# Four short runs of quarter-width products per pair of batches gathered into two

## The chip, the cores and the metric

The kernel runs on one core of one Trainium2 chip. The metric is the device time of one execution, in microseconds (us). TensorE multiplies, VectorE and ScalarE work on what it leaves in PSUM and prepare weights, GpSimd sets a few constants at the start, and SyncE's queue (SP) issues nearly all transfers.

## The reference, cut to what matters

Eight batches of 256 tokens with 1024 features go through four layers, each added to the residual stream:

```python
x = x + (x @ W0.T + 2 * lora(x, gates(x @ Wr.T)))       # 8 experts of rank 16, top 2 of 8 logits
x = x + (x @ W1.T + b1 + coeff[b] * (x @ (2 * mask[b] - 1)))
x = x + x @ W2[ids[b]].T                                # a weight per adapter
x = x + (x @ B3[ids[b]].T) @ A3[ids[b]].T               # adapter of rank 16
```

The router's logits `x @ Wr.T` (8 columns) decide which two experts of layer 0 a token uses. The projections `x @ B3[id].T` (16 columns) are the first half of layer 3. These two small products, both in float32, are what the change moves.

## The kernel before, in words

The residual stream is kept transposed, features on partitions, in K = 8 blocks of 128 features by T = 256 tokens. float32 operands of the large products are split into a high and a low float32r part, and a product is taken as high x high + high x low + low x high. `three` (lines 408 to 423) does so for the two batches of a pair at once, 512 tokens wide: 16 products with the weight's high part (L412, L413), then 8 with its low part (L420). `two` (425 to 439) does it for one batch: 8 products of the high part with both parts of x (L428), then 8 of 256 tokens with the low part (L436). Each takes callbacks: `early`, `mid` (between the high and the low part) and `late` (behind the low part) put other products of TensorE at these places.

The batches are taken in four pairs, q = 0 to 3. A pair is a stream of units, one weight block of 128 x 1024 each: one unit A (all experts' first factors, 128 rows), 8 units L0 (output block m), 16 units L1 and 16 units L2 (block m, batch j of the pair). Units are numbered through: with pair 0, A is 0, L0 is 1 to 8, L1 is 9 to 24, L2 is 25 to 40, so that unit (m, j) = (4, 1) of layer 2 is 34, (6, 0) is 37, and pair 1's A is 41. `slot(i)` issues a unit's work in a fixed order: the load of unit i + 9, the evacuation of the last unit's products, the high and low parts (L184 on ScalarE, L191 on VectorE) of units about four ahead, the addition of the identity to later blocks (`fold`, L159 on VectorE, five and six units ahead), other side work, and then `main(i)`, the unit's products. The order on each engine is the order in which the program is written; nothing is planned at run time. Loads of weights, masks, and inputs share ten buffers of the pool "raw"; a load waits on SP's queue until its buffer is let go by its last reader.

Logits and projections have few output columns. They are padded to 32, a quarter of the array: `logits(b, h)` takes half of batch b's eight feature blocks, four products that go to the four quarters of the array (L259), from the raw input; two halves finish a batch. `proj(b, h)` does the same for the adapter's projections from the finished x of layer 2 (L467). The four quarters' results are four partial sums, on 32 partitions each. The logits' are copied (L265), transposed (L270), and summed by `router` on VectorE. The projections' are split (`proj_sum`, L90 on ScalarE and L91 on VectorE) and summed by a product with a constant (`sums`, L369 and L370), which `rank` puts into the middle of the next pair's first L0 unit. Products with float32 operands stand in the trace as two records each.

For a pair that has a next one, with n = 2q + 2 the next pair's first batch, `main` puts them as follows: in the middle of unit (4, 1) of layer 2 the first halves of both batches' projections and all logits of batch n; in the middle of (6, 0) the logits of n + 1; in the middle of the next A the second half of the first batch's projections; behind that A the second half of the other's. The results lie in buffers of the PSUM pool "aux", four of 512 floats by 128 partitions. At the start the first pair's logits come as the input comes, and the last pair has places of its own.

Of the kernel before, what the change touches and what calls it, by code (L numbers as in the profile page):

```python
# [8 lines left out]
F32 = mybir.dt.float32  # L9
# [6 lines left out]
P = 128  # L16
NB = 8          # batches
T = 256         # tokens of a batch
K = 8           # blocks of 128 features
E = 8           # experts / adapters  # L20
R = 16          # rank
LOAD_AHEAD = 9  # weight blocks loaded, and prepared, ahead of their products
PREP_AHEAD = 4
MERGE_AHEAD = (6, 7)    # layer 1's blocks merged before the layer: the first pair's, the others'
W1_BUFS = 3
RAW_BUFS = 10
WARM = 9        # products that raise the tensor engine's clock
# prepared later, so that the vector engine is free where layer 2 waits for layer 1's results
# [4 lines left out]
def kernel(ctx: ExitStack, tc: tile.TileContext, x, lang, coeff, ids,  # L33
                           mask, w0, wr, la, lb, w1, b1, w2, a3, b3, out):
    """The residual stream is kept transposed (features on partitions), so that each
    layer's output is the next one's moving operand. float32 operands are split
    exactly into two float32r parts (hi: 12 bits, lo: the rest)."""
    nc = tc.nc
# [11 lines left out]
    aux = ctx.enter_context(tc.tile_pool(name="aux", bufs=4, space=PS))  # L50
# [4 lines left out]
    # ---- small constants  # L55
    xraw = {}

    def load_x(b, h, parts=1):
        """Half of batch b's input."""
        t = rawp.tile([P, K // 2, T], F32, tag="raw", name=f"x{b}_{h}")  # L60
        n = K // 2 // parts
        for i in range(parts):
            c = slice(i * n, (i + 1) * n)
            nc.sync.dma_start(t[:, c, :], x[b, :, h * K // 2 + i * n:h * K // 2 + (i + 1) * n, :])
        xraw[b, h] = t

    # the router's weights: 8 columns and 24 of zeros, a quarter of the array's
# [8 lines left out]
    # the sum over the array's quarters, of R rows each, as three copies  # L76
# [11 lines left out]
    # ---- splits  # L88
# [19 lines left out]
    # ---- the stream of weight blocks, in the order of use  # L108
    units = []
    for q in range(NB // 2):  # L110
        units.append(("A", q, 0, 0))
        units += [("L0", q, m, 0) for m in range(K)]
        units += [("L1", q, m, j) for m in range(K) for j in range(2)]
        order = [(m, j) for m in range(K) for j in range(2)]
        if q == NB // 2 - 1:        # the last pair's first batch ends sooner
            order[-6:] = [(m, j) for j in range(2) for m in range(K - 3, K)]
        units += [("L2", q, m, j) for m, j in order]
    raws, ws, w1raw = {}, {}, {}

    def parts(i):  # L120
        # the first blocks come in two parts
        n = 2 if i < 2 else 1
        return [slice(j * K // n, (j + 1) * K // n) for j in range(n)]
# [26 lines left out]
    # a block's preparation in four steps, on two engines in turns  # L150
# [6 lines left out]
    def add_identity(w, m):  # L157
        """The residual, in the block where inputs and outputs are the same."""
        nc.vector.tensor_tensor(w[:, m, :], w[:, m, :], ident, ALU.add)  # L159
# [43 lines left out]
    # first blocks, ahead of the other constants  # L203
# [26 lines left out]
    def constants():  # L230
        # 5 where the expert is the batch's language; ids below 0 match none
        lang_f = cst.tile([P, NB], F32, name="lang_f")
        nc.vector.tensor_scalar(lang_f, lang_i, -1.0, float(E), ALU.mult, ALU.add)
        nc.vector.tensor_tensor(bias, rev.to_broadcast([P, NB, E]),
                                lang_f.rearrange("p (b o) -> p b o", o=1)
                                      .to_broadcast([P, NB, E]), ALU.is_equal)
        nc.vector.tensor_scalar(bias, bias, 5.0, None, ALU.mult)
        nc.vector.tensor_scalar(c2, c_sb, 2.0, None, ALU.mult)
        nc.vector.tensor_scalar(negc, c_sb, -1.0, None, ALU.mult)
        # adapters as an index: from the end below 0, then held in range  # L240
        neg = cst.tile([1, NB], F32, name="neg")
        idf = cst.tile([1, NB], F32, name="idf")
        nc.vector.tensor_scalar(neg, ids_raw, 0.0, float(E), ALU.is_lt, ALU.mult)
        nc.vector.tensor_tensor(idf, ids_raw, neg, ALU.add)
        nc.vector.tensor_scalar(ids_sb, idf, 0.0, float(E - 1), ALU.max, ALU.min)

    # ---- layer 0's router, from logits [16 = hi|lo, 512 tokens]
# [4 lines left out]
    def logits(b, h):  # L252
        """Half of batch b's logits in float32, four blocks of features at a time in the
        quarters of the array."""
        q, j = divmod(b, 2)
        if (j, h) == (0, 0):
            pls[q] = aux.tile([P, 512], F32, tag="aux", name=f"pl{q}")
        for g in range(4):
            nc.tensor.matmul(pls[q][32 * g:32 * g + 32, j * T:(j + 1) * T],  # L259
                             wrs[:, 4 * h + g, :], xraw[b, h][:, g, :],  # L260
                             start=(h == 0), stop=(h == 1))
# [11 lines left out]
    def router(q, pt):  # L273
# [31 lines left out]
        # 2 (the scaling) over 1 + e, and e times that  # L305
# [28 lines left out]
    # ---- layer 3, per batch  # L334
# [20 lines left out]
    def proj_sum(b, pb):  # L355
        """The sum over the quarters, three times."""
        pr = aux.tile([P, 512], F32, tag="aux", name=f"pr{b}")
        if b == NB - 1:
            # in one step, as nothing else is left to do meanwhile
            raw = gp.tile([P, T], F32, tag="pbraw", name="pbraw")  # L360
            nc.scalar.copy(raw, pb[:, :T])
            return pr, lambda: nc.tensor.matmul(pr[:96, :T], sel3_raw, raw, start=True,
                                                stop=True)
# [9 lines left out]
    def third(b, pb):  # L373
        """The projections' rows as hi, lo and hi again."""
        rt = l3p.tile([96, T], FR, tag="rt", name=f"rt{b}")
        nc.scalar.copy(rt, pb[:96, :T])
        nc.vector.tensor_tensor(rt[32:64, :], pb[32:64, :T], f32(rt[32:64, :]), ALU.subtract)
        return rt
# [17 lines left out]
    # ---- products  # L396
# [11 lines left out]
    def three(po, hi, lo, xhi, xlo, last=True, early=(), mid=(), late=()):  # L408
        """po = (hi + lo)^T (xhi + xlo), over the K blocks of 128; early, mid, late:
        other work in between."""  # L410
# [14 lines left out]
    def two(po, hi, lo, xhl, early=(), mid=(), late=()):  # L425
        """As three(), for one batch: hi with x's both parts at once, into po's halves."""
# [21 lines left out]
    summed = []     # units whose two halves' sum is under way  # L448
    done = []       # what is left of the units that have gone through the tensor engine
# [11 lines left out]
    def proj(b, h):  # L461
        """Half of batch b's projections onto its adapter's rank, in float32 and the
        quarters of the array."""
# [14 lines left out]
    def first_products():  # L478
        """The first two units' products and the first logits, as the input comes in."""
# [20 lines left out]
        for j in range(2):  # L500
# [15 lines left out]
            # both halves stay open, for the experts' part, in one group that batch 0 starts  # L516
# [11 lines left out]
    def main(i):  # L528
        """Unit i on the tensor engine."""
# [6 lines left out]
        if kind == "A":  # L536
            xhi, xlo = x0[q]
            ph = aux.tile([P, 512], F32, tag="aux", name="ph")
            three(ph, hi, lo, xhi, xlo, mid=[lambda: proj(b - 2, 1)],
                  late=[lambda: proj(b - 1, 1)])  # L540
            phs[q] = ph
        elif kind == "L0":
# [12 lines left out]
            if m == 1:  # L555
                def gate_now():
                    gates[q] = gate(gxs.pop(q), phs.pop(q))
                # the first gates come later than the others
# [15 lines left out]
        else:  # L574
            xh = hls[2, b]
            po = ps.tile([P, 512], F32, tag="mm", name=f"po2_{b}_{m}")
            if (m, j) == (4, 1):
                mid = [lambda: proj(b - 1, 0), lambda: proj(b, 0)]
            if q < NB // 2 - 1:
                n = 2 * q + 2  # L580
                if (m, j) == (4, 1):
                    mid += [lambda: logits(n, 0), lambda: logits(n, 1)]
                if (m, j) == (6, 0):
                    mid = [lambda: logits(n + 1, 0), lambda: logits(n + 1, 1)]
# [4 lines left out]
            else:  # L589
                if (m, j) == (K - 3, 1):  # L590
                    mid = [lambda: proj(b - 1, 1)]
# [4 lines left out]
            if i == len(units) - 1:  # L596
                # its sum is waited for at once
# [10 lines left out]
    nxt = []        # work for the vector engine once the scalar engine's is done  # L608

    def side(i):  # L610
        """Other loads and preparations beside unit i's products."""
# [19 lines left out]
    # the tensor engine's clock rises while the first blocks come in  # L631
# [8 lines left out]
    # the slots in which layer 1's weights are merged: the more in layer 0's, which leave the  # L640
    # vector engine time
# [8 lines left out]
    def slot(i):  # L650
        """Unit i's products, beside the evacuation of those before it and the
        preparation of those after it."""
# [14 lines left out]
        # the next products wait for the last ones' results: nothing between  # L667
# [28 lines left out]
    def evacuate(between=None):  # L696
        """Products (and bias) split into the next ones' operand."""
        items = done[:]
        done.clear()
        # those summed beside the last unit, then those complete on PSUM  # L700
# [27 lines left out]
    # the last batch's end: half of the residual joins on the tensor engine, so that two  # L728
    # engines can take the sums
# [81 lines left out]
```

## Time and profile before

| | us |
|---|---|
| Median of 3 runs | 628.63 (628.33 to 628.91) |
| Span of the profiled execution | 627.1 |
| Median less that span | 1.5 |
| TensorE busy, of the span | 618.9 (99%) |
| TensorE loading weights | 521.9 (83%) |
| VectorE busy | 460.6 (73%) |
| ScalarE busy | 362.9 (58%) |
| L467, 128 records of 32 x 256 | 9.9 |
| L259, 128 records of 32 x 256 | 9.5 |
| Clock granted to TensorE, mean | 0.997 of full speed |

The span goes from the first to the last instruction of one profiled execution on the core; the runs' time holds what lies around it as well. PE is TensorE's products and PEld its weight loads, which lie beside products. DVE is VectorE and ACT ScalarE; SPq is the queue of SyncE. A product's modelled end lies after the next one's start, so the sum of busy times counts some time twice; the distance from start to start is what a product costs. In a row of the timeline, "x8" is the number of records merged into it. "128*32" is the weight's shape, "128x256 f32" that of the moving operand. What stands in brackets behind a row is the engine's idle time before it, and who ended that.

### The profile page before, as it was taken

To read this page: it belongs to the slowest core of one execution; us is meant where nothing else is said; L and a number is where in the kernel's file an instruction comes from. 1 tells how busy PE (TensorE), PEld (TensorE's weight loads), DVE (VectorE), ACT (ScalarE), POOL (GpSimd) and SP (SyncE) were. 2 spreads that over 40 slices of the span, in tenths; PEclk is the share of its full clock that TensorE was granted. 3 is DMA by queue.
4 is the path that set the end of the run, shared out by engine and by line. 5 is a ranking of instruction groups with operands and counts; after the bars stand their busy time and mean duration, and the time that the engine had idled before them with its cause. 6 is when DMAs were issued, how large, how long until landed. Compare 5 with 4: busy or idle time off the path is not lost.

```text
span 627.1 us, 9247 instructions
## 1 busy us (share of the span) xinstructions
PE 618.9 (99%) x3458; PEld 521.9 (83%) x3458; DVE 460.6 (73%) x800; ACT 362.9 (58%) x552; POOL 1.0 (0%) x14
## 2 busy tenths in 40 slices
PE   8999999999999999999999999999999999999996
PEld 6888888888788888888878888888787888888885
DVE  6685898766657799777666689967775678987642
ACT  5375797565354498655435558865534446975521
POOL 0000000000000000000000000000000000000000
PEclk9999999999999999999999999999999999999998
DMA  8974575668725776476842778647774358765104
GB/s 272 397 229 153 201 269 174 208 203 270 250 72 168 234 268 199 138 247 220 310 136 74 203 240 276 186 138 247 240 272 134 121 182 259 247 199 164 39 0 135
DMA packets 38815, 125.01 MB, mean 199 GB/s; under 512 B 4722, under 2 KB 5874, under 8 KB 38770
## 3 DMA queue, kind: packets, MB, share of 16 engines
q1 hardware_dynamic: 38626, 124.15, 60.4%
q8 instruction: 27, 0.44, 0.3%
q10 hardware_dynamic: 144, 0.26, 0.1%
q14 instruction: 18, 0.15, 0.1%
HBM read 116.01 MB, written 8.39 MB: 198 GB/s over the span
## 4 chain that ended last, share of the span: by engine, by line
PE 98%; DMA 1%; SPq 0%; DVE 0%; ACT 0%; DVEq 0%; issue 0%
PE po L428 37%; PE po L436 20%; PE po L412 9%; PE po L420 9%; PE po L413 9%; PE pb L467 1%; PE po L454 1%; PE po L455 1%; PE po L456 1%; PE pl L259 1%; PE po L388 1%; PE ph L420 1%; PE ph L413 1%; PE ph L412 1%; DMA raw<-in_la 1%; PE ph L489 0%
## 5 line engine op out<-in xcount | busy, mean ns | idle before, releaser
L428 PE MATMUL po<-hl,whi 128*128 128x512 f32 x1016 | 254.5, 392 | 0.0
L428 PEld LDWEIGHTS po<-hl,whi 128*128 128x128 f32 x1016 | 182.9, 189 | 32.9
L191 DVE TENSOR_TENSOR wlo<-raw,whi 128x1024 fp32r<-128x1024 f32 (+1 forms) x166 | 199.0, 1205 | 1.8 <-ACT whi L184 1.8
L184 ACT CAST whi<-raw 128x1024 fp32r<-128x1024 f32 (+1 forms) x166 | 172.4, 1039 | 10.5 <-DVE raw L159 8.1
L436 PEld LDWEIGHTS po<-hl,wlo 128*128 128x128 f32 x1016 | 137.7, 190 | 12.2 <-issue 3.3
L436 PE MATMUL po<-hl,wlo 128*128 128x256 f32 x1016 | 142.7, 283 | 0.0
L412 PE MATMUL po<-x0hi,whi 128*128 128x512 f32 x248 | 97.1, 392 | 0.0
L413 PE MATMUL po<-x0lo,whi 128*128 128x512 f32 x248 | 96.7, 390 | 0.0
L174 DVE TENSOR_TENSOR raw<-raw,w 128x1024 f32<-128x1024 f32 x64 | 78.1, 1221 | 3.6 <-ACT raw L154 2.6
L154 ACT ACTIVATE raw<-raw,negc,c 128x1024 f32<-128x1024 int32 x64 | 79.7, 1245 | 0.0
L711 ACT COPY xt<-po 128x256 f32<-128x256 f32 x63 | 23.4, 372 | 87.2 <-PE po L436 87.2
L720 DVE TENSOR_TENSOR xt<-po,xt 128x256 f32<-128x256 f32 x63 | 26.7, 423 | 50.6 <-ACT xt L711 50.3
L420 PE MATMUL po<-x0hi,wlo 128*128 128x512 f32 x248 | 62.3, 393 | 0.0
L704 ACT CAST hl<-po 128x256 fp32r<-128x256 f32 x64 | 20.5, 376 | 71.6 <-PE po L456 71.5
L718 DVE TENSOR_TENSOR hl<-po,hl 128x256 fp32r<-128x256 f32 x64 | 23.8, 420 | 46.1 <-ACT hl L704 40.7
L412 PEld LDWEIGHTS po<-x0hi,whi 128*128 128x128 f32 x248 | 46.6, 188 | 11.1 <-issue 1.2
L413 PEld LDWEIGHTS po<-x0lo,whi 128*128 128x128 f32 x248 | 46.6, 188 | 9.8
L420 PEld LDWEIGHTS po<-x0hi,wlo 128*128 128x128 f32 x248 | 45.4, 188 | 8.8
L714 ACT ACTIVATE sum<-po,b_sb 128x256 f32<-128x256 f32 x64 | 30.4, 475 | 23.4 <-PE po L436 23.1
L720 DVE TENSOR_TENSOR sum<-po,sum 128x256 f32<-128x256 f32 x64 | 26.8, 419 | 12.7 <-ACT sum L714 12.6
L718 DVE TENSOR_TENSOR hl<-sum,hl 128x256 fp32r<-128x256 f32 x64 | 26.8, 419 | 4.6 <-ACT hl L704 4.6
L704 ACT CAST hl<-sum 128x256 fp32r<-128x256 f32 x64 | 25.6, 400 | 7.6 <-DVE sum L720 7.6
(116 smaller groups left out, 379.9 us busy)
## 6 DMA issues: line engine op xcount, KB each, us to landing
raw<-in_w SPq DMA_DIRECT2D x95, 512.0 KB, 4.3
raw<-in_mask SPq DMA_DIRECT2D x64, 512.0 KB, 5.4
w<-in_w SPq DMA_DIRECT2D x32, 512.0 KB, 4.6
out<-xt SPq DMA_DIRECT2D x31, 256.0 KB, 3.1
x<-in_x SPq DMA_DIRECT2D x12, 512.0 KB, 4.4
a3raw<-in_a SPq DMA_DIRECT2D x8, 384.0 KB, 3.6
x<-in_x SPq DMA_DIRECT2D x8, 256.0 KB, 5.8
raw<-in_la SPq DMA_DIRECT2D x3, 512.0 KB, 3.6
```

The costliest lines, as they stand in the source:

```text
L154: nc.scalar.activation(f32(raws[i]), raws[i], AF.Identity, bias=negc[:, b:b + 1], scale=c2[:, b:b + 1])
L174: nc.vector.tensor_tensor(s, s, w1raw[q, m], ALU.add)
L184: nc.scalar.copy(hi[:, c], source(i)[:, c])
L191: nc.vector.tensor_tensor(lo[:, c], source(i)[:, c], f32(ws[i])[:, c], ALU.subtract)
L412: nc.tensor.matmul(po, hi[:, k, :], xhi[:, k, :], start=(k == 0), stop=False)
L413: nc.tensor.matmul(po, hi[:, k, :], xlo[:, k, :], start=False, stop=False)
L420: nc.tensor.matmul(po, lo[:, k, :], xhi[:, k, :], start=False, stop=(last and k == K - 1))
L428: nc.tensor.matmul(po, hi[:, k, :], xhl[:, k].rearrange("p h t -> p (h t)"), start=(k == 0), stop=False)
L436: nc.tensor.matmul(po[:, :T], lo[:, k, :], xhl[:, k, 0, :], start=False, stop=(k == K - 1))
L704: nc.scalar.copy(hi, p)
L718: nc.vector.tensor_tensor(lo, p, f32(hi), ALU.subtract)
L720: nc.vector.tensor_tensor(xs, p[:, :T], xs, ALU.add)
```

## The change

For the first three pairs all logits of the next pair, of both batches, go into the middle of unit (6, 0), and nothing into (4, 1). All projections of both batches go behind the next unit A, nothing into its middle: `proj(b, None)` takes all eight blocks of a batch in one go, and ends with `proj_sum` as the second half did. The start, and the last pair with its places (4, 1), (5, 1) and the end, stay. The rest of the diff takes out comments and blank text.

```diff
     def proj(b, h):
+        if h is None:
+            pbs[b] = aux.tile([P, 512], F32, tag="aux", name=f"pb{b}")
+            for k in range(K):
+                g = k % 4
+                nc.tensor.matmul(pbs[b][32 * g:32 * g + 32, :T], l3[b][1][:, k, :],
+                                 xts[b][:, k, :], start=(k < 4), stop=(k >= 4))
+            prs[b], sums[b] = proj_sum(b, pbs.pop(b))
+            return
         if h == 0:
             pbs[b] = aux.tile([P, 512], F32, tag="aux", name=f"pb{b}")
...
         if kind == "A":
             xhi, xlo = x0[q]
             ph = aux.tile([P, 512], F32, tag="aux", name="ph")
-            three(ph, hi, lo, xhi, xlo, mid=[lambda: proj(b - 2, 1)],
-                  late=[lambda: proj(b - 1, 1)])
+            three(ph, hi, lo, xhi, xlo, late=[lambda: proj(b - 2, None), lambda: proj(b - 1, None)])
             phs[q] = ph
...
             po = ps.tile([P, 512], F32, tag="mm", name=f"po2_{b}_{m}")
-            if (m, j) == (4, 1):
-                mid = [lambda: proj(b - 1, 0), lambda: proj(b, 0)]
             if q < NB // 2 - 1:
                 n = 2 * q + 2
-                if (m, j) == (4, 1):
-                    mid += [lambda: logits(n, 0), lambda: logits(n, 1)]
                 if (m, j) == (6, 0):
-                    mid = [lambda: logits(n + 1, 0), lambda: logits(n + 1, 1)]
+                    mid = [lambda: [logits(bb, h) for bb in (n, n + 1) for h in range(2)]]
                 if (m, j) == (6, 1):
                     l2s[q + 1] = logits_by_token(q + 1)
                 if (m, j) == (7, 0):
                     mid = [l2s[q + 1][1]]
             else:
+                if (m, j) == (4, 1):
+                    mid = [lambda: proj(b - 1, 0), lambda: proj(b, 0)]
                 if (m, j) == (K - 3, 1):
                     mid = [lambda: proj(b - 1, 1)]
```

The buffers follow from the new order: a batch's projection buffer in "aux" is now taken behind A, where it was held from (4, 1) on, and the raw buffers of batch n's input are held up to (6, 0).

## The prediction

> **What bounds the kernel now.** I read the page's busy row first, then the chain that ended last.
>
> ```profile
> PE 618.9 (99%) x3458; PEld 521.9 (83%) x3458; DVE 460.6 (73%) x800; ACT 362.9 (58%) x552; POOL 1.0 (0%) x14
> PE 98%; DMA 1%; SPq 0%; DVE 0%; ACT 0%; DVEq 0%; issue 0%
> ```
>
> TensorE is busy for 99% of the span and makes up 98% of the chain. So a change counts here only by what it does to the distance between one product's start and the next on TensorE. Busy time can't show that distance, since a product's modelled end overlaps its successor; start times can. The timeline of TensorE around the first pair's layer 2 has these rows (start, length, engine, line, tiles, form, records):
>
> ```profile
> 136.52 2.00 PE L428 MATMUL po<-hl,whi 128*128 128x512 f32 x8
> 138.46 1.07 PE L467 MATMUL pb<-xt,b 128*32 128x256 f32 x16
> 139.34 1.05 PE L259 MATMUL pl<-x,wrs 128*32 128x256 f32 x16
> ...
> 141.37 2.00 PE L428 MATMUL po<-hl,whi 128*128 128x512 f32 x8
> ...
> 144.16 2.00 PE L428 MATMUL po<-hl,whi 128*128 128x512 f32 x8
> ...
> 146.96 2.00 PE L428 MATMUL po<-hl,whi 128*128 128x512 f32 x8
> 148.89 1.07 PE L259 MATMUL pl<-x,wrs 128*32 128x256 f32 x16
> ...
> 150.95 2.00 PE L428 MATMUL po<-hl,whi 128*128 128x512 f32 x8
> ```
>
> A unit of layer 2 without anything in it lasts from 144.16 to 146.96, 2.80 us. The unit that holds eight projection and eight logits products (each stands in the trace as two records, so 16 + 16) lasts from 136.52 to 141.37, 4.85 us: 2.05 more. The unit with eight logits products (16 records) lasts from 146.96 to 150.95, 3.99 us: 1.19 more. Sixteen further records thus cost 0.86, or 0.054 us each, and the run itself costs 1.19 - 16 x 0.054 = 0.33 us, however long it is. I call a stretch of quarter-width products (the form 128*32) between full-width ones a run, and the 0.33 its fixed price.
>
> The two short runs, of four projection products each, check this. They stand in the next unit, A:
>
> ```profile
> 159.76 0.40 PE L412 MATMUL ph<-x0hi,whi 128*128 128x512 f32 x1
> ...
> 163.19 0.39 PE L413 MATMUL ph<-x0lo,whi 128*128 128x512 f32 x1
> 163.51 0.64 PE L467 MATMUL pb<-xt,b 128*32 128x256 f32 x8
> 164.08 2.11 PE L420 MATMUL ph<-x0hi,wlo 128*128 128x512 f32 x8
> 166.12 0.64 PE L467 MATMUL pb<-xt,b 128*32 128x256 f32 x8
> 166.69 0.50 PE L412 MATMUL po<-x0hi,whi 128*128 128x512 f32 x1
> 167.03 0.39 PE L413 MATMUL po<-x0lo,whi 128*128 128x512 f32 x1
> ```
>
> From 159.76 to 163.19 are 15 starts, 0.229 apart. Unit A's 24 products would take 24 x 0.229 = 5.49 us; it lasts until 166.69, 6.93 us. The first product behind the second run is followed after 0.34 (167.03) and not 0.23, another 0.11. So the two runs cost 1.55, 0.77 each; the rule above gives 0.33 + 8 x 0.054 = 0.76. The fixed price shows at the edges: 0.32 us from the last full-width start to the run's first (163.19 to 163.51) and not 0.23, and 0.34 behind the run's first successor; the rest is between the run's last records and that successor.
>
> **The change, part by part.**
>
> *Runs on TensorE.* Per pair that has a next one (three of the four) the runs are now 32, 16, 8 and 8 records. After the change they are 32 (all logits, in unit (6,0) of layer 2) and 32 (all projections, behind A's products). No product goes or comes: 64 records on both sides. Before: 2.05 + 1.19 + 1.55 = 4.79 us. After: 2 x 2.05 = 4.10 us. The difference, 0.69, is two fixed prices (2 x 0.33 = 0.67). I take 0.67 per pair; the other two pairs show the same row lengths (1.07, 1.05, 1.07, 0.64, 0.64), so 3 x 0.67 = 2.0 us. The start-up and the last pair keep their runs.
>
> A rule speaks against this. The Trainium skill's "TensorE: Matmul & The Clock Gate", section "Measured speedup vs the span model", prices a pack of products in different parts of the array at one product's duration plus about 4 ns for each further one. With the trace's 0.379 us for L467's records that is 0.39 per pack of four. If packs simply stood one behind another, the 16 packs of a pair would cost 16 x 0.39 = 6.3 us in two runs as in four, and the saving would be 0. The rows say otherwise: 16 records, four packs, take 139.34 - 138.46 = 0.88 us, 0.22 each. Packs of one run overlap; it is the edges that are paid in full. So 2.0 by the rows, 0 by the rule; I take the rows.
>
> *A semaphore wait within a run.* In the changed kernel's order of instructions, batch b - 1's first projection waits for its adapter's load and for its PSUM buffer, and one of these waits became an instruction of its own on TensorE's queue, amid the run. Both are long fulfilled: the load by a whole layer, the buffer (the logits' before) by the scalar engine's copy of them, three units earlier. Such instructions exist already:
>
> ```profile
> L412 PEldq EVENT_SEMAPHORE  x4: 51/51/51, 38.3 to 56.5; - x4
> ```
>
> The first, at 38.3, lies between products that start at 37.96, 38.18, 38.41 and 38.64: no gap, as the queue runs ahead. None in the trace lies within a quarter-width run. From both sides: nothing, or, if the run falls into two, one more fixed price, 0.33 per pair and 1.0 in all. I take 0, by the row, and keep 1.0 for the range.
>
> *Later projections, and who waits.* The first projections move from mid A to its end, so their splits move too. Now:
>
> ```profile
> 164.27 0.37 ACT L90 CAST pbhi<-pb 128x256 fp32r<-128x256 f32 x1 [0.44 <-PE pb L467]
> 166.85 0.37 ACT L90 CAST pbhi<-pb 128x256 fp32r<-128x256 f32 x1 [2.21 <-PE pb L467]
> 167.26 0.42 DVE L91 TENSOR_TENSOR pblo<-pb,pbhi 128x256 fp32r<-128x256 f32 x1 [1.11 <-ACT pbhi L90]
> ```
>
> The scalar engine waits for the second projections anyway; nothing stands between its two splits. On the new clock, A's end comes at 166.12 - 2.05 + 0.86 - 0.77 = 164.16 (logits gone from (4,1), more of them in (6,0), no run in mid A). The run's halves finish at about 165.4 and 166.3 (start, 0.88 per half, some 0.4 for a product to end). Then the splits: ScalarE to 166.7, VectorE to about 167.1, which is 0.5 sooner than now (167.68). What stands behind them, the high and low parts of later weights, moves up with them. The sums (L369, L370) come 16 products after the run, at 164.16 + 1.85 + 16 x 0.229 = 169.7: 2.6 us of cover. Without it each microsecond would be paid on TensorE, three times. The batch's last block of layer 2, which the last projection reads, is done at 164.48 - 1.2 = 163.3, and is read at 165.5.
>
> *One batch's logits three units later.* No DMA instruction moves, but two of the four "raw" buffers (of ten) that hold the next inputs are let go later, and the weights behind them on SP's queue change buffers. Now:
>
> ```profile
> SPq L144 <- PE pl L259: 11.3, 7, 2.8
> DMA to landing us min/median/max: 3.3/4.7/6.9
> ```
>
> The second row is of these loads, 130 to 170 us. In the changed order two loads (units 44, 45) wait for VectorE's low parts of units 38 and 39 instead of the logits: issued at about 144.7 - 2.05 = 142.6 and 144.3, not 140.0 and 140.5. The next two (46, 47) wait for the logits: about 147.2 and 147.6, not 144.7 and 146.4. Their first reader is VectorE's addition of the identity (L159), at 153.0, 155.8, 159.1 and 165.5 now, 1.2 sooner then. With the slowest landing, 6.9, they are there at 149.5, 151.2, 154.1 and 154.5, against 151.8, 154.6, 157.9 and 164.3: at least 2.3 us of cover. The next mask block gets its buffer sooner. I price this at 0.
>
> *Sum.* The profiled execution has a span of 627.1 us; the median of the runs is 628.63, 1.5 more, which lies around the span and is not touched. 627.1 - 2.0 = 625.1 of span; 628.63 - 2.0 = 626.6 us.
>
> **Rivals.** *The run breaks at the semaphore.* For: no row shows such a wait within a run. Against: the row above, and that TensorE's queue is ahead by a whole pack (the weights of the second pack load at the first one's start). Time: 626.6 + 1.0 = 627.6; half broken, 627.1.
>
> *The saving goes elsewhere:* the sums wait for the later splits, or packs of different tiles overlap less than the 32-record row shows. For: three engines in a row stand between the run and the sums. Against: 2.6 us of cover, and that row mixes two tiles already. It needs 0.67 per pair: 628.6.
>
> *Slower: a weight block comes late.* Its place is SP's wait for the logits in (6,0). Six blocks and masks then follow each other closely, and in this stretch DMA already moves 400 GB/s at times. It decides from a landing 2.3 us beyond the slowest seen, as VectorE then stands at L159 with all later low parts behind it; beyond that, TensorE has up to two units' prepared weights left. With 1.3 us lost per pair: 628.63 - 2.0 + 3.9 = 630.5. Against it: no product of this stretch waits now, and landings of 10 us and more would be needed.
>
> That the change doesn't do what it says is excluded: the order of instructions has two runs per pair.
>
> **How the numbers follow.** The forecast has 0.80, the broken run 0.09, the lost saving 0.06, the late block 0.05. A measurement of this kernel tells 0.2% (1.26 us) from no change: faster means below 627.4. The forecast and half of the broken-run cases are: 0.84. Same: the other half and the lost saving, 0.10. Slower: the late block and a bit of the lost saving, 0.06. The range: below, six prices of 0.36 and 0.4 for the spread of the runs (628.33 to 628.91), 626.0; above, the fully broken run, 627.6.
>
> **What would show it.** Timeline of TensorE: units (4,1) at 2.80 us and (6,0) at 4.85; one row of 32 L259 records near 146.8 and one of projections behind A's products near 164.2, both with starts 0.22 apart per pack; unit A plus run 24 x 0.229 + 2.05. Wrong would be a step over 0.25 within the run, L369 waiting for ACT or DVE, or L428, L412 and L420 starting late behind a VectorE low part.

## The result, and the profile after

The changed kernel takes 626.89 us (median of 8 runs, 626.56 to 627.42) against 628.95 for the kernel before (8 runs, 628.33 to 630.51); the ratio is 0.9965, with an interval of 0.9955 to 0.9974. The forecast was 626.6. The profiled execution's span went from 627.1 to 624.9 us, 2.2 us less, where 2.0 was forecast. Beside later kernels the changed one was run again: 626.68 us, span 625.0, ratio 0.9964 (0.9950 to 0.9978).

The page's busy row and chain after:

```profile
PE 616.8 (99%) x3458; PEld 522.9 (84%) x3458; DVE 460.8 (74%) x800; ACT 363.0 (58%) x552; POOL 1.0 (0%) x14
PE 98%; DMA 1%; SPq 0%; DVE 0%; ACT 0%; DVEq 0%; issue 0%
```

TensorE has the same 3458 records and is as full as before; 2.1 us of its time are gone, and nothing took their place in the chain. TensorE's timeline, after, at the places that the prediction read (start, length, engine, line, tiles, form, records):

```profile
136.55 2.00 PE L428 MATMUL po<-hl,whi 128*128 128x512 f32 x8
...
139.34 2.00 PE L428 MATMUL po<-hl,whi 128*128 128x512 f32 x8
...
144.93 2.00 PE L428 MATMUL po<-hl,whi 128*128 128x512 f32 x8
146.86 1.93 PE L259 MATMUL pl<-x,wrs 128*32 128x256 f32 x32
148.73 1.21 PE L436 MATMUL po<-hl,wlo 128*128 128x256 f32 x8
149.78 2.00 PE L428 MATMUL po<-hl,whi 128*128 128x512 f32 x8
...
162.24 1.98 PE L420 MATMUL ph<-x0hi,wlo 128*128 128x512 f32 x8
164.15 1.93 PE L468 MATMUL pb<-xt,b 128*32 128x256 f32 x32
166.01 0.50 PE L412 MATMUL po<-x0hi,whi 128*128 128x512 f32 x1
```

Unit (4,1), which held sixteen products, is bare: 139.34 - 136.55 = 2.79. Unit (6,0) lasts 149.78 - 144.93 = 4.85, as (4,1) did before with as many records. Two rows of 32 stand where rows of 32, 16, 8 and 8 stood. The best measure of a pair is the distance between the first product of layer 1 (L428) in one pair and in the next, since it holds everything once and nothing of the start. Before, these rows are

```profile
66.70 1.99 PE L428 MATMUL po<-hl,whi 128*128 128x512 f32 x8
...
219.10 1.99 PE L428 MATMUL po<-hl,whi 128*128 128x512 f32 x8
```

and after

```profile
66.73 1.99 PE L428 MATMUL po<-hl,whi 128*128 128x512 f32 x8
...
218.42 1.99 PE L428 MATMUL po<-hl,whi 128*128 128x512 f32 x8
```

so a pair's period went from 152.40 to 151.69, by 0.71 us. The next two periods of each trace are the same to the hundredth. The first products of layer 1 stand at nearly the same time: all of the gain is in the periods, and 3 x 0.71 = 2.1 of the 2.2.

### The profile page after: what moved, and what is told of

The parts are those of the page before. It is cut to its first block, busy times and chain, and to the rows that moved or that the text cites. A ratio compares the mean times of both kernels' runs of the same rounds, so it can differ in the third digit from the quotient of the medians.

```text
span 624.9 us, 9250 instructions
## 1 busy us (share of the span) xinstructions
PE 616.8 (99%) x3458; PEld 522.9 (84%) x3458; DVE 460.8 (74%) x800; ACT 363.0 (58%) x552; POOL 1.0 (0%) x14
## 4 chain that ended last, share of the span: by engine, by line
PE 98%; DMA 1%; SPq 0%; DVE 0%; ACT 0%; DVEq 0%; issue 0%
PE po L428 37%; PE po L436 20%; PE po L412 9%; PE po L420 9%; PE po L413 9%; PE po L454 1%; PE po L455 1%; PE po L456 1%; PE pl L259 1%; PE po L388 1%; PE pb L468 1%; PE ph L413 1%; PE ph L412 1%; PE ph L420 1%; DMA raw<-in_la 1%; PE ph L497 0%
## 5 line engine op out<-in xcount | busy, mean ns | idle before, releaser
L428 PE MATMUL po<-hl,whi 128*128 128x512 f32 x1016 | 254.5, 392 | 0.0
L428 PEld LDWEIGHTS po<-hl,whi 128*128 128x128 f32 x1016 | 182.9, 189 | 32.9
L412 PE MATMUL po<-x0hi,whi 128*128 128x512 f32 x248 | 97.1, 392 | 0.0
L412 PEld LDWEIGHTS po<-x0hi,whi 128*128 128x128 f32 x248 | 46.5, 188 | 11.1 <-issue 1.2
```

The source lines that it names most:

```text
L412: nc.tensor.matmul(po, hi[:, k, :], xhi[:, k, :], start=(k == 0), stop=False)
L428: nc.tensor.matmul(po, hi[:, k, :], xhl[:, k].rearrange("p h t -> p (h t)"), start=(k == 0), stop=False)
```

## The experiments

**One part alone, and the opposite.** Theory: a run (a stretch of quarter-width products between full-width ones) has a fixed price of about a third of a microsecond on TensorE, wherever it stands and however long it is. Rivals: the gain came from one of the places, or from what the moves did to other engines. The first kernel gathers the logits only. Against the changed kernel:

```diff
-            three(ph, hi, lo, xhi, xlo, late=[lambda: proj(b - 2, None), lambda: proj(b - 1, None)])
+            three(ph, hi, lo, xhi, xlo, mid=[lambda: proj(b - 2, 1)],
+                  late=[lambda: proj(b - 1, 1)])
...
+                if (m, j) == (4, 1):
+                    mid = [lambda: proj(b - 1, 0), lambda: proj(b, 0)]
```

> Only the logits are gathered (all in unit (6,0)); the projections stay as before, first halves in (4,1), second halves in and behind A. Runs per pair: 16, 32, 8, 8 records, four as before. Theory (a fixed price of 0.33 us per run, whatever its place or length): no change, span within 0.2 us of the kernel before, ratio 1.000; unit (4,1) 3.99 us and (6,0) 4.85 us, the reverse of before. Rival (the gain comes from what the logits' place does to ScalarE, VectorE and the loads): a gain of 0.7 us or more, ratio 0.9989 or less.

Measured: ratio 0.9994 (0.9985 to 1.0002), span 627.2. Its timeline has unit (4,1) at 140.69 - 136.70 = 3.99 us,

```profile
136.70 2.00 PE L428 MATMUL po<-hl,whi 128*128 128x512 f32 x8
138.63 1.07 PE L475 MATMUL pb<-xt,b 128*32 128x256 f32 x16
...
140.69 1.55 PE L428 MATMUL po<-hl,whi 128*128 128x512 f32 x6
```

and two starts of layer 1

```profile
66.88 1.99 PE L428 MATMUL po<-hl,whi 128*128 128x512 f32 x8
...
219.28 1.99 PE L428 MATMUL po<-hl,whi 128*128 128x512 f32 x8
```

so that the period is 152.40, that of the kernel before. Eight products moved by three units, and the buffers of the inputs with them, and nothing came of it, since the number of runs stayed four. The second kernel gathers the projections only:

```diff
             if q < NB // 2 - 1:
                 n = 2 * q + 2
+                if (m, j) == (4, 1):
+                    mid = [lambda: logits(n, 0), lambda: logits(n, 1)]
                 if (m, j) == (6, 0):
-                    mid = [lambda: [logits(bb, h) for bb in (n, n + 1) for h in range(2)]]
+                    mid = [lambda: logits(n + 1, 0), lambda: logits(n + 1, 1)]
```

> Only the projections are gathered (all behind A); the logits stay at their two places. Runs per pair: 16, 16, 32, three where there were four. Theory: one fixed price per pair, 3 x 0.34 = 1.0 us faster than before, ratio 0.9984. Rival (all of the gain is the emptied middle of A and the later split): 2.0 us faster, as with the whole change. Rival (a denser pack in a longer run): 0.5 us or less.

Measured: ratio 0.9984 (0.9973 to 0.9994), span 626.4. Its two starts of layer 1 are

```profile
67.15 1.99 PE L428 MATMUL po<-hl,whi 128*128 128x512 f32 x8
...
219.18 1.99 PE L428 MATMUL po<-hl,whi 128*128 128x512 f32 x8
```

The period is 152.03: 0.37 less than before for one run less. The span fell by 0.7 and not by 3 x 0.37 = 1.1, because this execution reached layer 1 later, at 67.15 and not 66.70. The intervals of these two ratios still reach what the rivals forecast (0.9989 with the logits alone, 0.5 us or 0.9992 with the projections alone); it is the periods that rule them out. The third kernel has as many products in eight runs:

```diff
-                if (m, j) == (6, 0):
-                    mid = [lambda: [logits(bb, h) for bb in (n, n + 1) for h in range(2)]]
+                at_ = {(4, 1): (n, 0), (5, 0): (n, 1), (5, 1): (n + 1, 0), (6, 0): (n + 1, 1)}
+                if (m, j) in at_:
+                    mid = [lambda: logits(*at_[m, j])]
+                if (m, j) == (6, 1):
+                    mid = [lambda: proj(b - 1, 0)]
+                if (m, j) == (7, 1):
+                    mid = [lambda: proj(b, 0)]
```

with the second halves of the projections in and behind A, as before the change.

> The same 64 records per pair in eight runs of 8 records, each in a unit of its own: (4,1), (5,0), (5,1), (6,0) for the logits' halves, (6,1) and (7,1) for the projections' first halves, A's middle and end for the second ones. Theory: four fixed prices more per pair than before, 3 x 4 x 0.34 = 4.1 us slower than before (span 631.2), ratio 1.0065; each of these units 0.76 to 0.77 us longer than a bare one. Rival (records cost, not runs): no change. Rival (the price is the move from mid to end of A alone): no change.

Measured: ratio 1.0068 (1.0051 to 1.0085), span 631.3. Rows of its timeline, the first pair's first two such units and the two starts of layer 1:

```profile
66.92 1.99 PE L428 MATMUL po<-hl,whi 128*128 128x512 f32 x8
...
136.74 2.00 PE L428 MATMUL po<-hl,whi 128*128 128x512 f32 x8
138.67 0.64 PE L259 MATMUL pl<-x,wrs 128*32 128x256 f32 x8
...
140.30 2.00 PE L428 MATMUL po<-hl,whi 128*128 128x512 f32 x8
...
143.86 2.00 PE L428 MATMUL po<-hl,whi 128*128 128x512 f32 x8
...
220.67 1.08 PE L428 MATMUL po<-hl,whi 128*128 128x512 f32 x4
```

Each of these units lasts 3.56 us, 0.77 more than a bare one. The period is 153.75: 1.35 more than before for four runs more, 0.34 each. So for 2, 3, 4 and 8 runs of the same records a pair takes 151.69, 152.03, 152.40 and 153.75 us. That is close to a straight line in the number of runs, with steps of 0.34, 0.37 and 0.34 for each run more, and the two kernels with four runs, whose places differ, agree to the hundredth.

**What the price belongs to.** At a run's edges both the width and the type change: from float32r at full width to float32 at a quarter. The next kernel puts unread extra products into bare units of layer 2, in all pairs:

```diff
+            if m in (1, 2, 3):
+                mid = [lambda: probe(m, j, hi, xh)]
...
+    def probe(m, j, hi, xh):
+        dum = aux.tile([P, 512], F32, tag="aux", name="dum")
+        x = f32(xh[:, m, 0, :])
+        if (m, j) in ((1, 0), (3, 0)):
+            for g in range(4 * (m - 1) or 4):
+                c = 32 * (g % 4)
+                nc.tensor.matmul(dum[c:c + 32, :T], f32(hi[:, m, c:c + 32]), x,
+                                 start=(g < 4), stop=(g >= 4 * (m - 1) - 4))
+        elif (m, j) == (2, 0):
+            nc.tensor.matmul(dum[:, :T], f32(hi[:, m, :]), x, start=True, stop=True)
+        elif j == 1:
+            xb = xh[:, m, 0, :].bitcast(mybir.dt.bfloat16)[:, :T]
+            wb = hi[:, m, :].bitcast(mybir.dt.bfloat16)
+            if m == 1:
+                for g in range(4):
+                    nc.tensor.matmul(dum[32 * g:32 * g + 32, :T], wb[:, 32 * g:32 * g + 32], xb,
+                                     start=True, stop=True)
+            elif m == 2:
+                nc.tensor.matmul(dum[:, :T], wb[:, :P], xb, start=True, stop=True)
+            else:
+                for g in range(4):
+                    nc.tensor.matmul(dum[:32, :T], hi[:, m, 32 * g:32 * g + 32], xh[:, m, 0, :],
+                                     start=(g == 0), stop=(g == 3))
```

> The changed kernel with unread extra products in the middle of units m = 1 to 3 of layer 2, in all pairs: (1,0) one float32 quarter-width pack of four, (1,1) the same in bfloat16, (2,0) one full-width float32 product of 256 columns, (2,1) one full-width bfloat16 product, (3,0) two float32 quarter-width packs, (3,1) four float32r products of quarter width, all in the first quarter. A bare unit is 2.80 us. If the fixed price belongs to the change of width: +0.76, +0.44, +0.43, +0.11, +1.19, +0.76. If it belongs to float32 after float32r: +0.76, +0.11, +0.76, +0.11, +1.19, +0.43. Sum over four pairs: 14.8 us by width, 13.4 us by float32, on the changed kernel's span of 624.9.

TensorE's timeline of the first pair, from the first unit with a probe to the first without:

```profile
118.73 2.00 PE L428 MATMUL po<-hl,whi 128*128 128x512 f32 x8
120.66 0.64 PE L542 MATMUL dum<-hl,whi 128*32 128x256 f32 x8
...
122.29 2.00 PE L428 MATMUL po<-hl,whi 128*128 128x512 f32 x8
124.22 0.29 PE L551 MATMUL dum<-hl,whi 128*32 128x256 bf16 x4
...
125.50 2.00 PE L428 MATMUL po<-hl,whi 128*128 128x512 f32 x8
...
128.72 2.00 PE L428 MATMUL po<-hl,whi 128*128 128x512 f32 x8
...
131.64 2.00 PE L428 MATMUL po<-hl,whi 128*128 128x512 f32 x8
...
135.63 2.00 PE L428 MATMUL po<-hl,whi 128*128 128x512 f32 x8
137.47 0.64 PE L557 MATMUL dum<-hl,whi 128*32 128x256 f32 x4
...
138.90 2.00 PE L428 MATMUL po<-hl,whi 128*128 128x512 f32 x8
```

From one L428 to the next, less the bare 2.79:

| Unit | Probe | More, us | By width | By float32 |
|---|---|---|---|---|
| (1,0) | float32, one pack in four quarters | 0.77 | 0.76 | 0.76 |
| (1,1) | bfloat16, one pack in four quarters | 0.42 | 0.44 | 0.11 |
| (2,0) | float32, one product, full width | 0.43 | 0.43 | 0.76 |
| (2,1) | bfloat16, one product, full width | 0.13 | 0.11 | 0.11 |
| (3,0) | float32, two packs in four quarters | 1.20 | 1.19 | 1.19 |
| (3,1) | float32r, four products in the first quarter | 0.48 | 0.76 | 0.43 |

The second and third row decide against float32: bfloat16 in quarters pays the price, float32 at full width does not. (The 0.42 isn't four bfloat16 products one behind another: the row of four is 0.29 us long, and each of them 0.28.) But the last row missed: four products of 32 columns of float32r cost hardly more than 4 x 0.11. The probes' sum is 3.43 us per pair, 13.7 in all; the span grew by 640.3 - 624.9 = 15.4, of which 1.7 lies ahead of layer 1, which began at 68.46 and not 66.73. The expected sums, 14.8 by width and 13.4 by float32, decide nothing here: the 1.1 that is missing by width is the last probe's, and by float32 the misses of the second and third row cancel.

That row left two readings: the first quarter is spared, or float32r is. One more kernel asks, with another function in the probe's place:

```diff
+        quarters = {1: (0, 0, 0, 0), 2: (1, 1, 1, 1), 3: (0,) if j == 0 else (0, 1)}[m]
+        for n, g in enumerate(quarters):
+            nc.tensor.matmul(dum[32 * g:32 * g + 32, :T], w[:, 32 * n:32 * n + 32], x,
+                             start=True, stop=True)
```

where `w` and `x` are float32 for j = 0 and bfloat16 for j = 1.

> As the probe before, with other unread products of 32 columns in the middle of layer 2's units, 0.22 us per float32 record and 0.11 per bfloat16 product where nothing overlaps: (1,0) four float32 in the first quarter, (1,1) four bfloat16 in the first, (2,0) four float32 in the second, (2,1) four bfloat16 in the second, (3,0) one float32 in the first, (3,1) one bfloat16 in the first and one in the second. If any product of quarter width pays the fixed price (so that only float32r was spared it in the last probe): 1.73 + 0.33 = 2.06, 0.43 + 0.33 = 0.76, 2.06, 0.76, 0.76, 0.44. If the first quarter alone pays none: 1.73, 0.43, 2.06, 0.76, 0.43, 0.44.

```profile
117.53 2.00 PE L428 MATMUL po<-hl,whi 128*128 128x512 f32 x8
...
122.36 2.00 PE L428 MATMUL po<-hl,whi 128*128 128x512 f32 x8
...
125.89 2.00 PE L428 MATMUL po<-hl,whi 128*128 128x512 f32 x8
...
130.72 2.00 PE L428 MATMUL po<-hl,whi 128*128 128x512 f32 x8
...
134.25 2.00 PE L428 MATMUL po<-hl,whi 128*128 128x512 f32 x8
...
137.79 2.00 PE L428 MATMUL po<-hl,whi 128*128 128x512 f32 x8
...
141.00 0.40 PE L428 MATMUL po<-hl,whi 128*128 128x512 f32 x1
```

More than the bare 2.79, in the order of the units: 2.04, 0.74, 2.04, 0.74, 0.75, 0.42. The first reading of the expectation named 2.06, 0.76, 2.06, 0.76, 0.76, 0.44. So the first quarter pays as the second does, and even a single product pays; of what was tried, narrow float32r alone went free. Why float32r does was not tried further: it stood in the first quarter only, and its four products were added up in one result, where the four of the last probe each began a new one.

**The cover of the sums.** The prediction gave the splits behind the projections 2.6 us until the sums need them. This kernel takes the cover away:

```diff
-            three(ph, hi, lo, xhi, xlo, late=[lambda: proj(b - 2, None), lambda: proj(b - 1, None)])
+            three(ph, hi, lo, xhi, xlo, late=[lambda: proj(b - 2, None), lambda: proj(b - 1, None),
+                                                 lambda: rank(b - 2), lambda: rank(b - 1)])
...
-            if m == 0:
-                mid = [lambda: rank(b - 2), lambda: rank(b - 1)]
```

> The changed kernel with the quarters' sums (L369, L370) straight behind the projections' run, not 16 products later: the cover of the splits is gone. If the cover was needed: TensorE stands from the run's end until VectorE's second low part is done, 166.0 to 167.0 in pair 0, so some 1.0 us per pair, 3 us in all, span 628, and the wait names VectorE's L91. If TensorE doesn't wait for the splits (they are done sooner than the rows say): span 625.

Measured in a single run: 628.13 us, span 626.4, 1.4 more than the changed kernel beside it. Two rows of its waits, and TensorE's timeline behind the run:

```profile
PEld pr L369 <- ACT pbhi L90: 2.0, 6, 0.4
PEld pr L370 <- DVE pblo L91: 0.9, 3, 0.3
```

```profile
163.89 1.93 PE L468 MATMUL pb<-xt,b 128*32 128x256 f32 x32
165.75 0.36 PE L369 MATMUL pr<-pbhi,sel 128*96 128x256 f32 x1
...
166.80 0.36 PE L370 MATMUL pr<-pblo,sel 128*96 128x256 f32 x1
167.00 0.39 PE L412 MATMUL po<-x0hi,whi 128*128 128x512 f32 x1
```

TensorE does wait, as the first reading said, but the period (66.47 to 218.79) grew by 0.63 us, not by 1.0, and the span of 628 was not reached. Of the waiting, 2.0 us in all lie before L369, on ScalarE's splits, and 0.9 before L370, on VectorE's, which alone the expectation named. From the run's first start to L412 it takes 3.11 us and not 1.86, 1.25 more. The four sums are part of that and no longer stand in the next unit, where they took 0.47, and the slow 0.11 behind the run falls into the wait (L412 is followed after 0.23): 1.25 - 0.47 - 0.11 = 0.67, near the 0.63. The cover is needed, and its price was set too high since the sums fill a part of the wait.

**A faster version.** The count of runs can be lowered at both ends too:

```diff
-                if k % 4 == 0:
-                    logits(j, k // 4)
+                if j == 0 and k % 4 == 0:
+                    logits(j, k // 4)
+                if j == 1 and k == 4:
+                    logits(1, 0)
+                    logits(1, 1)
...
-                if (m, j) == (4, 1):
-                    mid = [lambda: proj(b - 1, 0), lambda: proj(b, 0)]
                 if (m, j) == (K - 3, 1):
-                    mid = [lambda: proj(b - 1, 1)]
+                    mid = [lambda: proj(b, 0), lambda: proj(b - 1, None)]
```

> The changed kernel once more, beside the next two: span 624.9, ratio to the kernel before 0.9965 to 0.9968 by every theory.

> The changed kernel with two more runs gathered where no pair follows: at the start both halves of batch 1's logits stand together in front of the fifth of its eight blocks, and in the last pair all early projections (both of batch 6, the first of batch 7) stand in unit (5,1), none in (4,1). Theory: two fixed prices less, 0.34 + 0.33 = 0.67 us faster than the changed kernel, span 624.2, ratio to before 0.9954. Rival for the start: the first products wait for the input there, so that only the last pair's 0.34 shows, span 624.6.

Measured: 626.06 us (median of 7), ratio to before 0.9963 (0.9952 to 0.9974), beside 626.68 and 0.9964 (0.9950 to 0.9978) for the changed kernel. Five of its seven runs took 625.80 to 626.06 us, below all five of the changed kernel's (626.47 to 626.77); the other two took 627.8 and 627.9, so that the intervals don't tell the two kernels apart. The profiles do: the span is 624.1 against 625.0. At the start, from batch 0's low products of the first L0 block (L501, at 13.68 in both) to the transposes of the logits (L270) it takes 20.14 - 13.68 = 6.46 us and not 20.47 - 13.68 = 6.79, 0.33 less, which the rival for the start had denied. In the last pair, from unit (4,0) to the unit behind (5,1), it takes 606.79 - 588.41 = 18.38 and not 607.46 - 588.73 = 18.73, 0.35 less, and the last pair's two places stand together (L475 and L468 in one run, with no full-width product between):

```profile
604.30 0.64 PE L475 MATMUL pb<-xt,b 128*32 128x256 f32 x8
604.76 1.05 PE L468 MATMUL pb<-xt,b 128*32 128x256 f32 x16
605.74 1.22 PE L436 MATMUL po<-hl,wlo 128*128 128x256 f32 x8
```

It is the fastest version that was run: its median is 0.62 us below that of the changed kernel, where 0.67 was expected.

## Why the prediction was right

*Runs.* The step held, with its price a little low: 0.33 predicted, 0.71 / 2 = 0.355 measured by the period, 0.37 for projections alone, and 0.34 where runs were added. Of the rest, 0.71 - 0.67 = 0.04 us per pair, about half stands in A's low products. Between A's two former runs they took 166.12 - 164.08 = 2.04 us; after the change they begin at 162.24 and the run at 164.15, 1.91. That is 0.13, of which 0.11 is the first successor, which the prediction counted, and about 0.02 a slower pace of the other products behind a run, which it did not. The other half is rounding: by its own rows it had 0.69, and it took two prices of 0.33.

*The rule of a pack's price* (the Trainium skill's "TensorE: Matmul & The Clock Gate", section "Measured speedup vs the span model") is one for a single pack of products; set end to end, as the prediction tried it, packs of 0.39 us would have given no saving. That was a use beyond the rule, and the runs decide for the rows: packs of one run follow each other in 0.22 us though each product lasts 0.379.

*The semaphore within the run* cost nothing. It is in the trace after, on TensorE's queue, once per pair:

```profile
L468 PEldq EVENT_SEMAPHORE  x3: 51/51/51, 164.2 to 467.5; - x3
```

The run that holds it takes 166.01 - 164.15 = 1.86 us to the next product, the logits' run without one 148.73 - 146.86 = 1.87. The rival of a broken run falls.

*The later splits* came as predicted; ScalarE's and VectorE's timelines after:

```profile
165.31 0.37 ACT L90 CAST pbhi<-pb 128x256 fp32r<-128x256 f32 x1 [2.66 <-PE pb L468]
166.18 0.37 ACT L90 CAST pbhi<-pb 128x256 fp32r<-128x256 f32 x1 [0.49 <-PE pb L468]
```

```profile
166.58 0.43 DVE L91 TENSOR_TENSOR pblo<-pb,pbhi 128x256 fp32r<-128x256 f32 x1 [0.44 <-ACT pbhi L90]
```

The last low part ends at 167.0 (predicted 167.1), and the first sum starts at 169.77 (predicted 169.7), so the cover was 2.8 us.

*The loads.* SP's wait for the logits shrank, and the slowest landing between 130 and 170 us grew little:

```profile
SPq L144 <- PE pl L259: 9.3, 4, 2.8
DMA to landing us min/median/max: 3.2/4.1/7.2
```

No product of this stretch waited for a weight. That two blocks are asked for 2.7 and 3.9 us later, and the next two 2.8 and 1.6, cost nothing here and in the kernel with the logits alone. Whether a still later place would have cost something was not tried.

## What to carry to other kernels

On a full TensorE, count the stretches of quarter-width products, not only the products: each stretch of float32 or bfloat16 ones between full-width ones cost about a third of a microsecond here, so small products that are not urgent belong together, as far as buffers and those who wait for them allow. Read such prices from start to start in the timeline, around one stretch and beside a unit without it, and check by varying their number. When gathering moves a result later, look for the products that separate it from its reader: here sixteen of them, and without them 0.63 us per pair of the 0.71 were lost again.

## What was not expected of the hardware

Four products of 32 columns in float32r, in the first quarter, cost 0.48 us, near four times the 0.11 of a full-width product of 256 tokens, and paid no fixed price; four in bfloat16 in the same quarter cost 0.74, and a single one in float32 0.75. The price thus goes with quarter width in float32 and bfloat16 and not with narrow weights as such. It is also nearly the same for a single product (0.75 - 0.43 = 0.32, with the 0.43 of the float32 product at full width) as for runs of four to sixteen (0.33 to 0.34).
